# A graph network on one core: the gated layer's tables made in the attention layer's last stretches

## The chip, the cores and the metric

The kernel runs on one core of a Trainium2 chip. The metric is the device time of the whole program in microseconds (us). Five engines work side by side, each with a queue of its own: PE (matmuls; PEld are its weight loads), DVE (vector operations), ACT (activations and copies), POOL (here mostly indirect gathers) and SP (issues transfers). ACT issues transfers too. All of them synchronise by semaphores.

## The reference

Four graph layers on N = 3125 nodes with 128 features and E = 50000 edges, sorted by destination; after each, the input is added and the rows are normalised.

```python
# 0: three graph convolutions; norm = dinv[src] * edge_weight * dinv[dst]
for W, b in ((W1, b1), (W2, b2), (W3, b3)):
    x = relu(segment_sum((x @ W)[src] * norm, dst) + b)     # with a loop on each node
# 1: attention, 4 heads of 32
e = sum(leaky_relu((x @ W_l)[dst] + (x @ W_r)[src], 0.2) * att)
alpha = softmax of e over the edges of one dst
x = segment_sum((x @ W_r)[src] * alpha, dst) + bias
# 2: gated
z = concatenate([x[dst], x[src], edge_attr])
x = x + segment_sum(sigmoid(z @ W_f + b_f) * softplus(z @ W_s + b_s), dst)
# 3: ten graph convolutions, each with a layer norm and gelu, then a residual branch
```

## The kernel before

**Tiles and stretches.** The nodes are 25 tiles of 128 rows, kept in SBUF as `x`. The edges are 392 chunks of 128, cut into 28 stretches (`NS`) of 14 chunks (`SC`); a stretch has four blocks of 4, 4, 3 and 3 chunks (`BLOCKS`). Since the edges are sorted by destination, a stretch touches few rows, and after the stretches 6, 12, 18 and 24 (`WHOLE`) five more tiles (`CK`) are complete each time, 20 in all.

**Layer 0** (`l0_sorted`) is done with a dense adjacency matrix of seven banks of columns. It is built in SBUF strips out of one-hot matrices (pool `l0_hot`, tiles `of_pair`, `heavy`), used at once for the first convolution and written to memory (`bank<-strip`). The second and third convolutions stream it back in pieces of five tiles (`adj_k<-bank`, pool `l0_adj`, four buffers), which lies in SBUF where pools opened earlier have been closed. Between the two, `load_nodes` fetches `x` again and `attention.prepare` fetches and writes small things for the next layer (`s_left`, `s_dst_pad`, `wide`, `order`), all on SP.

**Layer 1**, attention (`l1_sorted`), runs as a pipeline over slots `(s, b)`, a stretch and a block of it. Its order is written out by hand: the recorders `pe_`, `ve`, `ac` and `sp` (class `InOrder`, line 189 in the profile) chain the instructions of an engine in the order in which the code issues them. POOL gathers the rows of sources (`xj`), PE brings `zT` together, ACT and DVE make `leaky`, PE the logits `e`, which go through memory (`s_logits`) to `near`; `weights` makes a maximum by scans and `w` by an exponential on ACT; `messages` (DVE, `msg`), `add_up` (PE, `sums`), `rows` and `finish` (write to `s_after`) follow three stretches later. The slots with `s >= 28` do only these last steps of the last stretches: a round is `weights(s-2)` at `b = 3`, then `messages(s-3)` at `b = 0`, `add_up` at `b = 1`, `rows` at `b = 2`, `finish` at `b = 3`. After the loop `x` is fetched again in one transfer of 25 tiles.

**Layer 2**, gated (`l2_sorted`), first prepares two tables in memory for all 25 tiles: `s2_to_src` (`row`, the product with the source's weights) and `s2_to_dst` (`parts`, the product with the destination's weights and the bias, split into three bfloat16 parts). Then it loops over the blocks of the stretches. POOL gathers `zj` from `s2_to_src` (three buffers of a stretch each; 42 gathers can run before the first buffer has to come free), PE makes `pz` out of the edges' attributes (`eaT`) and the rows of `s2_to_dst` (`td`, chosen by `of_node`, made from `drow`), DVE adds them to `z`, ACT and DVE make gate and softplus (`soft`, `gate`, `pz`), DVE `msg`, PE `sums`, and rows follow. From stretch 7 on, PE also does units of the last layer's first convolution (`sums<-adj_u,xs`, five matmuls each), added up by DVE (`columns`).

**Layer 3** (`l3`) is ten convolutions with streamed pieces of the adjacency, and isn't touched.

Of the kernel before, what the change touches and what calls it, by code (L numbers as in the profile page):

```python
# [9 lines left out]
F32 = mybir.dt.float32  # L10
# [8 lines left out]
P = 128  # L19
# [6 lines left out]
CK = 5  # L26
# [9 lines left out]
WHOLE = (6, 12, 18, 24)  # L36
CH = 20
# [11 lines left out]
def tile_gnn_stack(ctx: ExitStack, tc: tile.TileContext, a: dict, out: bass.AP):  # L49
# [96 lines left out]
    def load_nodes():  # L146
        nc.sync.dma_start(x, a["x"].rearrange("(t p) d -> p t d", p=P))
# [635 lines left out]
    def l0_sorted(edges, adj, attention):  # L783


        with (
# [13 lines left out]
            with (  # L800
                tc.tile_pool(name="l0_strips", bufs=2) as strips,
                tc.tile_pool(name="l0_hot", bufs=2) as hot,
            ):
                lanes.pin()
                edges.build(strips, hot, ps, adj, lambda b, strip: conv.sums(x, b, *layers[0], strip), ready)
                lanes.free()
            with (
# [3 lines left out]
                load_nodes()  # L811
# [249 lines left out]
    class Attention:  # L1061
# [15 lines left out]
        def prepare(self, scratch, ps, ve):  # L1077
# [11 lines left out]
            nc.sync.dma_start(self.left[NP:].rearrange("p a b -> p (a b)"), zero)  # L1089
            zero_f = scratch.tile([P, D], F32, name="zero_f")  # L1090
            nc.vector.memset(zero_f, 0.0)
            nc.sync.dma_start(self.before[NP:], zero_f)
            nc.sync.dma_start(self.after[NP - P:NP], zero_f)
            nc.sync.dma_start(self.logits[:, :NEAR], zero_f[:HEADS, :NEAR])
            nc.sync.dma_start(self.logits[:, NEAR + NCH * P:], zero_f[:HEADS, :NEAR])
            edge = scratch.tile([1, NEAR + 1], I32, name="edge")
            nc.vector.memset(edge, NP)
            nc.sync.dma_start(dst_pad[:, :NEAR + 1], edge)
            nc.sync.dma_start(dst_pad[:, NEAR + 1 + NCH * P:], edge)
            v = a["dst_r"]  # L1100
            nc.sync.dma_start(dst_pad[:, NEAR + 1:NEAR + 1 + NCH * P],
# [4 lines left out]
            nc.sync.dma_start(wide, bass.AP(tensor=dst_pad.tensor, offset=dst_pad.offset,  # L1106
# [6 lines left out]
            nc.sync.dma_start(order, bass.AP(tensor=v.tensor, offset=v.offset,  # L1113
                                             ap=[[SC, P], [SE, NS], [1, SC]]))
            v = a["src_r"]
            nc.sync.dma_start(self.src_o.rearrange("p (s c) -> p s c", c=SC), bass.AP(
# [52 lines left out]
    def l1_sorted(at):  # L1169
        right, left, before, after, local, logits = at.right, at.left, at.before, at.after, at.local, at.logits  # L1170
        fresh, src_o, dl, att, bias, apart, step = (at.fresh, at.src_o, at.dl, at.att, at.bias, at.apart, at.step)
        with (
# [5 lines left out]
            nc.vector.memset(eps, EPS)  # L1178
            with (
# [140 lines left out]

                NK = len(BLOCKS)
                load(0)
                select(0)
                for s in range(NS + 4):
                    for b in range(NK):
                        if b == 0 and s + 1 < NS:
                            load(s + 1)
# [24 lines left out]
                        if b == 3:  # L1352
                            if 0 <= s - 2 < NS:
                                weights(s - 2)
                            if 0 <= s - 3 < NS:
                                finish(s - 3)
                        if s < NS:
                            positive(s, b)
            nc.sync.dma_start(x, after[:NP].rearrange("(t p) d -> p t d", p=P))


    def l2_sorted(conv):
# [10 lines left out]
        with (  # L1373
# [7 lines left out]
            to_dst = dram.tile([NP + P, 3, 2 * D], BF16, name="s2_to_dst")  # L1381
            to_src = dram.tile([NP, 2 * D], F32, name="s2_to_src")
            before = dram.tile([NP + P, D], F32, name="s2_before")
            after = dram.tile([NP + P, D], F32, name="s2_after")
            local = dram.tile([NCH * P], BF16, name="s2_local")

# [10 lines left out]
            by_stretch = prep.tile([NS, SE], I32, name="by_stretch")  # L1397
            nc.sync.dma_start(by_stretch, a["dst_r"].rearrange("(s e) -> s e", e=SE))
            origin = one.tile([NS, len(BLOCKS)], F32, name="origin")
            lrow = prep.tile([NS, SE], BF16, name="lrow")  # L1400
            origin_i = one.tile([1, NCH], I32, name="origin_i")
            nc.sync.dma_start(origin_i, a["dst_c"][0:1, :])
            for b, (c0, n) in enumerate(BLOCKS):
                nc.vector.tensor_scalar_min(origin[:, b:b + 1], by_stretch[:, c0 * P:c0 * P + 1], float(N - 1))
                nc.vector.tensor_scalar(lrow[:, c0 * P:(c0 + n) * P], by_stretch[:, c0 * P:(c0 + n) * P],
                                        origin[:, b:b + 1], None, op0=OP.subtract)
            nc.vector.tensor_scalar(origin_i, origin_i, float(N - 1), 3.0, op0=OP.min, op1=OP.mult)
            nc.sync.dma_start(local.rearrange("(s e) -> s e", e=SE), lrow)
# [17 lines left out]
            w2 = one.tile([D, 3, 2, D], F32, name="w2")  # L1426
            for s, name in enumerate(("L2_gnn_W_f", "L2_gnn_W_s")):
                nc.scalar.dma_start(w2[:, :, s, :], a[name].rearrange("(r k) d -> k r d", k=D))
            b2 = one.tile([P, 2, D], F32, name="b2")
            for s, name in enumerate(("L2_gnn_b_f", "L2_gnn_b_s")):  # L1430
                v = a[name]
                nc.scalar.dma_start(b2[:, s, :], bass.AP(tensor=v.tensor, offset=v.offset, ap=[[0, P], [1, D]]))
# [6 lines left out]
            with tc.tile_pool(name="s2_ps0", bufs=4, space=PSUM) as ps:  # L1439
                xT = transposed_x(one, ps, conv.xs[0].rearrange("p t d -> p (t d)"))  # L1440
                def product(u, m, side):
                    pp = ps.tile([P, 2, 2 * D], F32, name="pp")[:, :m]
                    for q in range(m):
                        nc.tensor.matmul(pp[:, q, :], xT[:, (u + q) * P:(u + q + 1) * P],
                                         w2[:, side].rearrange("k s d -> k (s d)"), start=True, stop=True)
                    return pp


                for u in range(0, NT, 2):
                    m = min(2, NT - u)  # L1450
# [368 lines left out]
```

## Time and profile before

| what | value |
|---|---|
| median of 6 runs | 3546.76 us (3542.76 to 3549.2) |
| the profiled execution | 3532.18 us, span 3530.1 us |
| its mean granted clock of PE | 0.891 of full speed |
| PE busy | 2785.7 us (79% of the span) |
| DVE busy | 1645.0 us (47%) |
| ACT busy | 986.8 us (28%) |
| POOL busy | 821.1 us (23%) |
| layer 0: build and first convolution | to 364 us |
| layer 0: two streamed convolutions | to about 690 us |
| attention layer | to 1414.7 us |
| gated layer, preparation and first gathers | to 1512 us |
| gated layer, loop | to 2203 us |
| last layer | 2241 us to the end |

The profile is of one execution; it is 14.6 us shorter than the median of the runs. Times in it run from the start of the span. A line of the timeline has start, duration, engine, source line, operation, output and inputs, and in brackets how long the engine had been idle and what ended that. "issue" is idle time in which nothing that the profile shows was waited for; "remote" was ended by something that the trace doesn't hold. Source line 189 is the helper that records the hand-written order, so groups of that line are told apart by their tiles.

### The profile page before, as it was taken

Reading aid. Unit: us, or ns where it says so; the run is one execution under the profiler, and the core shown is the slowest. Engines: PE = TensorE matmul, PEld = TensorE weight load, DVE = VectorE, ACT = ScalarE, POOL = GpSimd, SP = SyncE. Lnnn points to the kernel's source line nnn. Section 1 sums busy time; section 2 is a strip of 40 time slices with the busy share of each in tenths; the row PEclk is TensorE's granted clock in tenths of the full one; section 3 lists DMA queues with packets and bytes.
Section 4 is the critical chain, followed back from the end, with each engine's and each line's share of the span. In section 5 each row is a group of like instructions: output and inputs, shape, how many; then the busy total and the mean of one; then the engine's idle time right before and its main releaser. Section 6 shows DMA issues by size and latency. Waiting matters only on the chain.

```text
span 3530.1 us, 33089 instructions
## 1 busy us (share of the span) xinstructions
PE 2785.7 (79%) x11223; PEld 1616.9 (46%) x11223; DVE 1645.0 (47%) x4368; ACT 986.8 (28%) x1491; POOL 821.1 (23%) x864
## 2 busy tenths in 40 slices
PE   2899899716656647356676677899999999999998
PEld 1666455403323324244454455455555555555554
DVE  6897112205545547466666667454232323232334
ACT  0333001202222222355555555232212122121212
POOL 3211000174555551445545452000000000000000
PEclk7899999857778778688888889999999999999999
DMA  2344987422222222655656565866766766666665
GB/s 56 113 160 163 306 278 247 152 57 78 72 68 82 80 69 60 200 157 153 204 172 200 173 193 166 265 203 200 237 208 213 227 219 221 217 215 217 223 211 176
DMA packets 413151, 609.90 MB, mean 173 GB/s; under 512 B 55434, under 2 KB 380312, under 8 KB 412956
## 3 DMA queue, kind: packets, MB, share of 16 engines
q1 hardware_dynamic: 366094, 520.33, 46.1%
q0 software_dynamic: 32320, 79.09, 8.2%
q10 hardware_dynamic: 14558, 8.27, 0.8%
q8 instruction: 91, 1.49, 0.2%
q14 instruction: 88, 0.72, 0.1%
HBM read 545.16 MB, written 62.61 MB: 172 GB/s over the span
## 4 chain that ended last, share of the span: by engine, by line
PE 44%; DVE 10%; issue 8%; another core or an unknown queue 4%; DMA 3%; ACT 1%; POOL 1%; SPq 1%; DVEq 0%; ACTq 0%
PE acc L691 34%; PE sums L189 3%; PE pz L189 3%; DVE z L189 2%; PE po L708 2%; DVE msg L189 1%; DVE pz L189 1%; DVE gate L189 1%; DVE of_edge L189 1%; PE zT L189 1%; PE e L189 1%; DMA drow<-s_local 1%; POOL xj L217 1%; SPq L189 0%
## 5 line engine op out<-in xcount | busy, mean ns | idle before, releaser
L691 PE MATMUL acc<-adj_k,xs 128*128 128x460 f32 (+1 forms) x2920 | 1120.9, 537 | 3.4 <-DMA adj_k<-bank 3.4
L691 PEld LDWEIGHTS acc<-adj_k,xs 128*128 128x128 f32 x2920 | 548.0, 190 | 503.0 <-issue 450.3
L217 POOL DMA_INDIRECT xj<-s_right,src_o x392 | 373.0, 951 | 624.5 <-ACT parts L1162 338.7
L217 POOL DMA_INDIRECT zj<-s_to_src,src_i x392 | 373.4, 953 | 364.6 <-DVE z L189 216.6
L691 PE MATMUL acc<-adj,xs 128*128 128x460 f32 (+1 forms) x1000 | 393.0, 543 | 15.2 <-DMA adj<-bank 15.2
L189 PE MATMUL pz<-w,eaT 128*128 128x256 f32 x784 | 276.2, 451 | 127.6 <-issue 97.1
L189 PE MATMUL sums<-msg,of_edge 128*128 128x132 f32 (+1 forms) x1568 | 236.0, 302 | 166.2 <-issue 138.6
L189 PEld LDWEIGHTS sums<-msg,of_edge 128*128 128x128 f32 x1568 | 214.4, 212 | 192.3 <-issue 147.5
L724 DVE SCALAR_TENSOR_TENSOR v<-po,dinv,three 128x128 f32<-128x128 f32 x250 | 72.3, 344 | 476.5 <-PE po L708 476.2
L691 PEld LDWEIGHTS acc<-adj,xs 128*128 128x128 f32 x1000 | 190.2, 191 | 202.3 <-issue 190.5
L189 PE MATMUL e<-leaky,att 128*4 128x512 f32 (+1 forms) x224 | 123.8, 638 | 148.8 <-issue 84.5
L189 PEld LDWEIGHTS pz<-w,eaT 128*128 128x128 f32 x784 | 145.8, 228 | 207.9 <-issue 135.9
L736 ACT ACTIVATE rs<-rs 128x4 f32<-128x4 f32 (+2 forms) x91 | 18.6, 205 | 681.7 <-DVE rs L735 681.6
L189 DVE TENSOR_TENSOR z<-pz,zj 128x1024 f32<-128x1024 f32 (+1 forms) x112 | 121.9, 1088 | 167.4 <-remote 139.7
L189 ACT ACTIVATE soft<-z 128x1024 f32<-128x1024 f32 (+1 forms) x112 | 106.2, 948 | 258.7 <-DVE z L189 196.6
L189 ACT ACTIVATE leaky<-zT 128x512 f32<-128x512 f32 (+1 forms) x112 | 60.5, 540 | 388.6 <-remote 184.8
L189 PEld LDWEIGHTS <-heavy 128*128 128x128 bf16 x1875 | 122.1, 101 | 83.8 <-issue 58.8
L189 PE MATMUL acc<-strip,x 128*128 128x460 f32 (+1 forms) x350 | 158.8, 562 | 0.0
L189 DVE TENSOR_TENSOR leaky<-zT,leaky 128x512 f32<-128x512 f32 (+1 forms) x112 | 69.0, 617 | 190.8 <-issue 143.0
L189 PE MATMUL side<-of_pair,heavy 128*128 128x125 bf16 x1875 | 134.6, 225 | 25.1 <-DVE heavy L189 19.7
L1710 ACT ACT_TABLE_LOAD x77 | 98.8, 1283 | 192.8 <-DVE v L1709 192.7
L189 DVE TENSOR_TENSOR heavy<-of_low,columns 128x2560 bf16<-128x2560 bf16 (+1 forms) x96 | 138.8, 1500 | 1.0
(220 smaller groups left out, 3244.5 us busy)
## 6 DMA issues: line engine op xcount, KB each, us to landing
adj_k<-bank SPq DMA_DIRECT2D x246, 1150.0 KB
adj_k<-bank SPq DMA_DIRECT2D x46, 912.5 KB
bank<-strip SPq DMA_DIRECT2D x6, 5750.0 KB
adj_u<-bank SPq DMA_DIRECT2D x24, 1150.0 KB
adj<-bank SPq DMA_DIRECT2D x14, 1150.0 KB
eaT<-in_ea_t SPq DMA_DIRECT2D x56, 256.0 KB
drow<-s_local SPq DMA_DIRECT2D x28, 448.0 KB
eaT<-in_ea_t SPq DMA_DIRECT2D x56, 192.0 KB
```

The lines of the kernel that those rows point to most:

```text
L189: ins = getattr(self.engine, name)(*args, **kwargs)
L217: after_writers(nc.gpsimd.indirect_dma_start(out=to, out_offset=None, in_=table[:NP, :], in_offset=bass.IndirectOffsetOnAxis(ap=index[:, c ...
L691: lanes.tensor.matmul(acc[:, :c1 - c0], xs[:, t, :], k[:, q, :c1 - c0], start=(t == begin), stop=(t == NT - 1))
L708: lanes.tensor.matmul(po[:, t - t0, :], self.aggT[:, t * P:(t + 1) * P], w, start=True, stop=True)
L724: lanes.vector.scalar_tensor_tensor(to[:, t - t0, :], sums[:, t - t0, :], dinv[:, t:t + 1], bias, op0=OP.mult, op1=OP.add)
L736: nc.scalar.activation(rs[:, :n], rs[:, :n], AF.Sqrt)
L1710: nc.scalar.activation(v, v, AF.Gelu)
```

## The change

There are four parts.

1. **Layer 0.** `l0_hot` is opened before `l0_strips`, so that the stream's four buffers lie in the memory of the one-hots, not of the strips. `load_nodes` and the transfers of `attention.prepare` go out on ACT's queue, not SP's.
2. **Attention layer.** A new class `Gated` holds the tables. Its weights (those of the gate negated) are fetched at the layer's start. SP fetches five finished tiles of `x` after the stretches in `WHOLE`, behind `finish`. In each slot with `s >= 28` a further pair of tiles begins its `steps`, five of them, one in each slot: transposes; the row; the bias and the product for the destination with its first part; second part; third part. They are put ahead of the attention's own work of the slot, in the same recorders, with `zT`'s buffers in PSUM and their transfers on ACT's queue. After the loop only five tiles of `x` are fetched.
3. **Gated layer, preparation.** It makes the tables of the last five tiles alone. `local`, the table behind `drow`, was written in the layer before.
4. **Gated layer, loop.** As the gate is negated, one operation over 256 columns a chunk serves gate and softplus, and ACT's exponential takes a scale of -1. `drow` comes as one transfer a stretch and `of_node` is made by one operation a stretch, at block 2. `load(s + 1)` moves from block 1 to block 0. `agg` is copied by ACT, and `u` reads PSUM. The unit is split, three matmuls at block 3 and two at the next block 0, and its addition moves from block 0 to block 1.

```diff
             with (
+                tc.tile_pool(name="l0_hot", bufs=2) as hot,
                 tc.tile_pool(name="l0_strips", bufs=2) as strips,
-                tc.tile_pool(name="l0_hot", bufs=2) as hot,
             ):
...
-                load_nodes()
+                load_nodes(nc.scalar)
...
-            nc.sync.dma_start(self.left[NP:].rearrange("p a b -> p (a b)"), zero)
+            nc.scalar.dma_start(self.left[NP:].rearrange("p a b -> p (a b)"), zero)
...
+    class Gated:
...
+        def steps(self, u, room, pe, ve, ac, queue):
+
+            m = min(2, NT - u)
+            w, pool = m * 2 * D, self.pool
+            ps = room()
+            for q in range(m):
+                pe.transpose(ps[:, q * P:(q + 1) * P], x[:, u + q, :], ident)
+            xT = pool.tile([D, 2 * P], F32, name="xT", bufs=3)
+            ac.activation(xT[:, :m * P], ps[:, :m * P], AF.Copy)
+            yield
+            ps = room()
+            for q in range(m):
+                pe.matmul(ps[:, q * 2 * D:(q + 1) * 2 * D], xT[:, q * P:(q + 1) * P],
+                          self.w[:, 1].rearrange("k s d -> k (s d)"), start=True, stop=True)
+            row = pool.tile([P, 2 * 2 * D], F32, name="row", bufs=2)
+            ac.activation(row[:, :w], ps[:, :w], AF.Copy)
+            queue.dma_start(self.to_src[u * P:(u + m) * P, :].rearrange("(t p) d -> p t d", p=P),
+                            row[:, :w].rearrange("p (t d) -> p t d", t=m))
+            yield
+            ps = room()
+            pe.matmul(ps[:, :w], self.ones, self.b.rearrange("p r s d -> p (r s d)")[:, :w],
+                      start=True, stop=False, skip_group_check=True)
+            for q in range(m):
+                pe.matmul(ps[:, q * 2 * D:(q + 1) * 2 * D], xT[:, q * P:(q + 1) * P],
+                          self.w[:, 0].rearrange("k s d -> k (s d)"), start=False, stop=(q == m - 1),
+                          skip_group_check=True)
+            parts = pool.tile([P, 2, 3, 2 * D], BF16, name="parts", bufs=3)[:, :m]
+            rest = pool.tile([P, 2, 2 * D], F32, name="rest", bufs=2)[:, :m]
+            of = ps[:, :w].rearrange("p (t d) -> p t d", t=m)
+            for i in range(3):
+                self.evict = ac.activation(parts[:, :, i], of, AF.Copy)
+                if i < 2:
+                    ve.tensor_sub(rest, of, parts[:, :, i])
+                    of = rest
+                    yield
+            queue.dma_start(self.to_dst[u * P:(u + m) * P].rearrange("(t p) i d -> p t i d", p=P), parts)
...
+                def fetch(j):
+                    sp.dma_start(x[:, j * CK:(j + 1) * CK, :],
+                                 after[j * CK * P:(j + 1) * CK * P].rearrange("(t p) d -> p t d", p=P))
...
                 for s in range(NS + 4):
                     for b in range(NK):
+                        if s >= NS:
+                            if 2 * turn < WHOLE_TILES:
+                                made.append(gated.steps(2 * turn, room, pe_, ve, ac, ac))
+                                turn += 1
+                            made = [g for g in made if next(g, made) is not made]
...
+                            if s - 2 in WHOLE:
+                                fetch(WHOLE.index(s - 2))
+                            if s == NS - 1:
+                                gated.places(ve, sp)
...
-            nc.sync.dma_start(x, after[:NP].rearrange("(t p) d -> p t d", p=P))
+            nc.sync.dma_start(x[:, WHOLE_TILES:, :], after[WHOLE_TILES * P:NP].rearrange("(t p) d -> p t d", p=P))
...
+            with tc.tile_pool(name="s2_ps0", bufs=6, space=PSUM) as ps:
+                made = [gated.steps(u, lambda: ps.tile([P, 512], F32, name="room"), nc.tensor, nc.vector,
+                                    nc.scalar, nc.sync) for u in range(WHOLE_TILES, NT, 2)]
+                while made:
+                    made = [g for g in made if next(g, made) is not made]
...
-                    ve.scalar_tensor_tensor(gate[:, :n], z[:, :n, :D], 0.0, soft[:, :n, :D],
-                                            op0=OP.min, op1=OP.subtract)
-                    ac.activation(gate[:, :n], gate[:, :n], AF.Exp)
-                    ve.scalar_tensor_tensor(soft[:, :n, D:], z[:, :n, D:], 0.0, soft[:, :n, D:],
-                                            op0=OP.max, op1=OP.add)
+                    ve.scalar_tensor_tensor(soft[:, :n], z[:, :n], 0.0, soft[:, :n], op0=OP.max, op1=OP.add)
+                    ac.activation(gate[:, :n], soft[:, :n, :D], AF.Exp, scale=-1.0)
...
-                ve.tensor_copy(agg, t["sums"])
+                ac.activation(agg, t["sums"], AF.Copy)
...
-                ve.scalar_tensor_tensor(u, t["xw"], 2.0, agg, op0=OP.mult, op1=OP.add)
+                ve.scalar_tensor_tensor(u, t["xw"], 2.0, t["sums"], op0=OP.mult, op1=OP.add)
...
-                    if b == 0 and s - 1 - FIRST in sums_of:
+                    if b == 1 and s - 1 - FIRST in sums_of:
                         add_unit(s - 1 - FIRST)
...
-                    if b == 1 and s + 1 < NS:
+                    if b == 0 and s + 1 < NS:
                         load(s + 1)
                     if k + 1 < len(steps):
                         products(*steps[k + 1])
+                    if b == 0 and s - 1 - FIRST in sums_of:
+                        unit(s - 1 - FIRST, room, range(3, CK))
...
-                    if k + 2 < len(steps):
-                        select(*steps[k + 2])
+                    if b == 2 and s + 1 < NS:
+                        select(s + 1)
...
                     if b == 3 and FIRST <= s < NS:
-                        unit(s - FIRST, ps_s.tile([P, 512], F32, name="sums"))
+                        room = ps_s.tile([P, 512], F32, name="sums")
+                        unit(s - FIRST, room, range(3))
```

## The prediction

> **What bounds the kernel now.** I read the page's slices first, then busy time by stage, then the timeline at the two seams that the change touches, then the groups and waits of the gated layer. In the slices (40 of 88 us each) PE is near full at the start and from slice 27 on; between, it is half busy and POOL, which issues the gathers, works too.
>
> ```profile
> PE   2899899716656647356676677899999999999998
> POOL 3211000174555551445545452000000000000000
> PEclk7899999857778778688888889999999999999999
> ```
>
> The last stage alone, 2400 to 3530 us, keeps PE busy for 1113.61 of 1130 us. The change leaves it as it is, so it can only win or lose before 2241 us: layer 0's turn (364 to 400), the attention layer's tail (1380 to 1415), the gated layer's preparation and first gathers (1415 to 1524) and its loop (to 2203).
>
> Stages (length; then busy time of PE, PEld, DVE, ACT, POOL with counts; granted clock, DMA share, GB/s):
>
> ```profile
> 360.00:380.00 20.00, 6.15 (x25) 3.59 (x23) 3.29 (x11) 0.48 (x1) 0.00 (x0) 0.67 0.70 175
> 380.00:400.00 20.00, 18.18 (x42) 8.72 (x43) 4.35 (x4) 0.00 (x0) 0.00 (x0) 0.90 1.07 379
> 1392.00:1402.00 10.00, 5.97 (x30) 5.78 (x30) 7.77 (x28) 0.50 (x2) 0.00 (x0) 0.67 0.13 32
> 1450.00:1500.00 50.00, 10.20 (x26) 6.71 (x25) 20.28 (x32) 20.73 (x34) 38.42 (x39) 0.59 0.63 197
> ```
>
> The turn loses PE for 14 us. The tail is nearly empty on ACT and DMA, and half empty on PE. While POOL gathers for the gated layer, the others do little. The timeline of these seams (start, duration, engine, instruction, idle time before and what ended it):
>
> ```profile
> 345.15 0.36 SPq L562 DMA_DIRECT2D bank<-strip  x1
> 363.88 0.77 SPq L147 DMA_DIRECT2D x<-in_x  x1
> 372.67 2.00 SPq L189 DMA_DIRECT2D adj_k<-bank  x1
> 380.23 6.00 PE L691 MATMUL acc<-adj_k,xs 128*128 128x460 f32 x10 [1.85 <-DMA adj_k<-bank]
> ...
> 1417.75 0.79 SPq L1359 DMA_DIRECT2D x<-s_after  x1
> 1426.41 3.84 PE L618 MATMUL xT_ps<-ident,x 128*128 128x128 f32 x16 [16.37 <-DMA x<-s_after]
> 1449.31 0.96 POOL L217 DMA_INDIRECT zj<-s_to_src,src_i  x1 [36.54 <-DVE rest L1466]
> 1511.66 1.22 DVE L189 TENSOR_TENSOR z<-pz,zj 128x1024 f32<-128x1024 f32 x1
> 1523.68 0.94 POOL L217 DMA_INDIRECT zj<-s_to_src,src_i  x1 [19.41 <-DVE z L189]
> ```
>
> From the attention layer's last write (1414.71) it takes 3.0 us until x is fetched, 8.7 until it is there, 22.9 of transposes, products and table rows until the first gather; 42 gathers then run 55 us, and 19.4 us pass before the 43rd. From there POOL sets the pace:
>
> ```profile
> 1895.58 0.96 DVE L189 TENSOR_TENSOR z<-pz,zj 128x768 f32<-128x768 f32 x1 [6.63 <-remote]
> 1900.46 0.96 DVE L189 TENSOR_TENSOR z<-pz,zj 128x768 f32<-128x768 f32 x1
> 1901.69 0.95 POOL L217 DMA_INDIRECT zj<-s_to_src,src_i  x1 [8.76 <-DVE z L189]
> ```
>
> A stretch is 14 gathers (17.2 us) and a gap: the next run waits for z of block 3, which frees the buffer, and z of block 2, 6.63 us idle before it, starts only 2.65 us after the run's end (1892.93). So a gap is 2.65 + 5.85 (z to z and its length) + 0.27 = 8.77 us.
>
> **The change part by part.** Sums are against the profiled execution, 3532.18 us; the median is 14.6 higher.
>
> *Layer 0's turn.* The stream's buffers move into the one-hots' memory, whose last reader ends at 344.42, so the first adj_k piece can be issued ahead of the bank write of 345.15, and the next three right behind it rather than after nodes and nine small transfers at 372.67. The bank write's packets end at 359.2; a piece lands every 3.15 us (1.15 MB at some 370 GB/s) and PE uses one in 3.93 (ten of 0.39). PE lost 13.85 us in the first window, 1.82 in the second and 2.1 to a cold clock (0.60 for 0.39, ten times): 17.8. I leave 5 of these, since x (1.6 MB, about 5 us), order (about 3) and wide (about 5) still share the DMA engines with the pieces, whose share was 1.07 right after: **-13** (-9 to -16). The Trainium skill's "Trainium Kernel Development and Optimization", Key Constraints, says that DMAs from the SP, ACT and POOL queues run on the same 16 engines, and that issuing from several saves only issue time; by it the move to ACT's queue is worth SP's 8.8 us from 363.88 to 372.67 at most, and the sum would be some 4 us higher. The trace's share of 1.07 agrees with it, while the memory move, which it does not touch, is the rest.
>
> *Attention layer, fetches.* Behind four of the 28 writes of finish, SP now waits for the write to land before it fetches five tiles of x. The nearest row is the 3.0 us from 1414.71 to 1417.75. Queued behind on SP are the next loads of hl and drow, and of_node waited up to 2.32 us for drow already. The stretch is 24.5 us and loads go two ahead, so I take 1 us each: **+4** (0 to +10). Its weights and indices (some 460 KB) are fetched at the layer's start, beside the first 84 gathers (704 to 802), where PE is busy for 7.92 of 50 us: nothing; without that cover, five issues of 0.5 us.
>
> *Attention layer, tail.* Ten pairs of tiles go through five steps in 14 slots from s=28 on, ahead of the attention's own work in the queues of PE, DVE and ACT. A full slot costs ACT three parts of 0.63, a row of 0.60, a copy of xT of 0.36 and two DMA issues of some 0.5 to 0.7: about 4.2 us; DVE two subtractions of 0.69; PE two transposes (0.2 each), four products and the bias product: 3.1 at full clock (0.22 a record), 6 at the cold one (0.53). A round of the old tail takes 11.9, 11.8 and 10.7 us and is a chain: msg on DVE 3.0, sums on PE 5.0 to 5.75, rows 2.2, scans 1.5, w on ACT 0.22. Half of its slots hide behind other engines: the slot before sums lies beside msg. The subtractions in the slots of rows, of weights and of msg stand in front on DVE and wait for PE and ACT: 2 to 4 us each. That makes 7 to 9 a round, less in the last, where no new pairs start: **+20**. The lower bound is ACT's own time, 10 x 4.2 = 42 for the 34 us that the tail had, less what starts in the idle time before 1380: +8. The upper is PE at its cold clock, 60 us of tables beside three times 5.4 of sums: 76 - 34 = +42.
>
> *Gated layer, preparation.* Twenty tiles' tables are already there. x's reload is 320 KB; the same size took 6 us from issue to use at 2215.84, where 1600 KB took 8.7: -2.5. Twenty-five transposes with their copies and 13 row products become five tiles in a chain of some 8 us: of 22.9 us some 10 stay, as the 1.6 MB write of s_before still shares the engines with the last rows. So the first gather comes about 15 us sooner (12 to 20). Parts now end far ahead of the gathers (1490.98 before), and drow of a stretch comes in one transfer: of_node waited 6.40 us for it until 1511.39. The gap behind the 42 gathers falls from 19.4 toward 8.77, for which I take 9 us (3 to 12): **-24** (-15 to -32).
>
> *Gated layer, loop.* Gate and softplus become one operation of 128x1024 (as z's 1.22) for 0.68 + 0.70; agg's copy of 0.28 leaves DVE for ACT; of_node's four operations of 0.35 become one of 0.69 in block 2. On the chain z to z in the gap that is -0.16, -0.28 and +0.34: -0.1. The unit's columns addition moves from block 0 to block 1, so that z of block 0 need not wait for five unit products (z at 1906.29 could come some 1.5 us sooner), and SP has three issues fewer a stretch. Much of this stands in waits. Over 25 stretches I take 0.3 each: **-8**, with -33 and +14 as ends (below).
>
> *Turn to the last layer.* The loads for it keep their order but for seven small ones that go ahead of the last writes; PE's idle time at 2241 ended on adj<-bank as before: 0 (-2 to +3).
>
> Sum: -13 + 4 + 20 - 24 - 8 = -21, so 3511 profiled and **3526** as a median.
>
> **The rivals.**
> *The tail costs more than the preparation gives (slower).* PE's clock was 0.67 at 60% busy; if it stays there, the tail is bound by PE at 6 us a slot: +42, and the last tables in the ACT ring delay the first gather, leaving -15. -13 + 4 + 42 - 15 - 8 = +10: 3557. With the preparation at -15 it decides from a tail of +32. For it: the in-order queues; against it: more work should lift the clock (1.00 at 400 to 450 us), and POOL is silent after 1342.6.
> *The loop goes into its shorter rhythm.* Some gaps are 5.4 to 7.3 us, where z of block 2 ran before the run's end (1687.62 us). With z of block 0 earlier, the 17 long gaps could lose 2 each: -33 for -8, 3501. Against it: z of block 2 waited even at 10 us after a run's start (1564.00 after 7.12).
> *The loop loses its short gaps.* The seven gaps under 8.1 sum to 13.6 us below 8.77; a chain longer by of_node's 0.69 could end them all: +14 for -8, 3548.
> *Earlier gathers serve nothing.* If PE and SP stay starved until the 42 gathers have landed and the gap behind them stays 19.4, and s_before's write holds the rows, the preparation gives 5: 3545, no change.
>
> **How the numbers follow.** Main case 0.45, with its terms' bounds 3505 to 3545: 0.40 faster, 0.05 same. Tail 0.20, slower. Short rhythm 0.15, faster. Lost gaps 0.08: 0.05 slower, 0.03 same. No use 0.12: 0.08 same, 0.03 slower, 0.01 faster. So faster 0.56, same 0.16, slower 0.28, where 0.2% (7 us) is about what a measurement of this kernel can tell from no change. The range, 3490 to 3560, holds all but the worse half of the tail's case and a short rhythm joined to a cheap tail.
>
> **What would show it.** PE's first layer-1 product soon after 366 us; rounds of msg in the tail 18 to 20 us apart, with DVE or ACT waiting for gated products; 15 us from the last write of the attention layer to the first zj gather for 34.6, and some 10 us before the 43rd gather for 19.4; gaps of about 8.5 us after. Wrong it would be if the rounds stay near 12 (gain larger) or exceed 25 (slower), or if periods in the loop move from 26 by over 1 us.

## The result and the profile after

On the chip of the profile the changed kernel takes 3515.99 us (median of 20 runs) against 3541.99 (46 runs): the ratio is 0.9929, 95% interval 0.9918 to 0.9939, which is 25 us less. Forecast were 20.8 us less. The profiled execution takes 3512.66 us (span 3510.9) for 3532.18. On a second kind of chip, told of below, the same change gains nothing: 1.0019 (1.0004 to 1.0033).

The slices of the page after (PE, POOL, granted clock):

```profile
PE   2899999726656558456777778899999999999998
POOL 3211000265556551355454541000000000000000
PEclk9999999857777779677888888999999999999999
```

PE is a tenth fuller in eight of the slices from 9 to 25, and a tenth emptier in one (the 14th); the last layer is as it was. The helper of the hand-written order is line 190 in the changed kernel, for 189 before. The stretches of before again (length; busy time of PE, PEld, DVE, ACT, POOL; clock, DMA share, GB/s):

```profile
360.00:380.00 20.00, 14.19 (x38) 6.45 (x36) 2.79 (x9) 0.00 (x0) 0.00 (x0) 0.91 1.04 298
380.00:400.00 20.00, 18.01 (x49) 9.41 (x50) 0.49 (x2) 0.55 (x1) 0.00 (x0) 0.91 1.08 377
1392.00:1402.00 10.00, 10.00 (x50) 8.00 (x51) 6.96 (x17) 4.44 (x9) 0.00 (x0) 0.83 0.50 164
1450.00:1500.00 50.00, 11.46 (x42) 7.46 (x42) 7.08 (x9) 9.35 (x12) 36.22 (x39) 0.57 0.58 174
```

In layer 0's turn PE is busy for 14.19 of 20 us, where it was 6.15. In the stretch of the attention layer's tail, where PE was busy for 5.97 of 10 us, it is now busy for all 10 (in the rest of the tail, 1334 to 1430, for 64 to 89% of the time), and ACT works there for 4.44 us and not 0.50. During the gated layer's first gathers DVE and ACT have lost most of the tables' work. The timeline at the seams:

```profile
340.14 0.36 SPq L190 DMA_DIRECT2D adj_k<-bank  x1
359.32 4.02 PE L692 MATMUL acc<-adj_k,xs 128*128 128x460 f32 x10
371.73 5.82 PE L692 MATMUL acc<-adj_k,xs 128*128 128x460 f32 x10 [2.39 <-DMA adj_k<-bank]
...
1431.25 0.40 SPq L1458 DMA_DIRECT2D x<-s_after  x1
1452.19 0.98 POOL L218 DMA_INDIRECT zj<-s_to_src,src_i  x1 [14.68 <-DMA s_to_dst<-parts]
1514.48 0.95 POOL L218 DMA_INDIRECT zj<-s_to_src,src_i  x1 [9.91 <-DVE z L190]
```

Milestones read off both timelines, in us:

| from, to | before | after | change |
|---|---|---|---|
| start to the last group of one-hot products | 344.1 | 339.8 | -4.3 |
| to the last group of products for attention's tables | 332.4 | 325.5 | -6.9 |
| to the first xj gather | 7.3 | 10.1 | +2.8 |
| to the end of the last xj gather | 658.8 | 659.3 | +0.5 |
| to the last y of the attention layer (tail) | 71.8 | 94.3 | +22.6 |
| to the first zj gather | 35.0 | 23.1 | -11.8 |
| to the 43rd zj gather | 74.4 | 62.3 | -12.1 |
| to the last run of gathers (24 periods) | 609.9 | 594.0 | -16.0 |
| to the last layer's first streamed product | 107.8 | 112.0 | +4.2 |
| to the end | 1288.7 | 1290.5 | +1.8 |

These sum to -19.2, the difference of the spans. Each column is read off one execution.

### The profile page after: what moved, and what is told of

It reads as the page before. It is cut to its first block, busy times and chain, and to the rows that moved or that the text cites. A ratio compares the mean times of both kernels' runs of the same rounds, so it can differ in the third digit from the quotient of the medians.

```text
span 3510.9 us, 32732 instructions
## 1 busy us (share of the span) xinstructions
PE 2808.8 (80%) x11249; PEld 1615.4 (46%) x11249; DVE 1597.8 (46%) x4127; ACT 1004.9 (29%) x1539; POOL 823.9 (23%) x864
## 4 chain that ended last, share of the span: by engine, by line
PE 52%; issue 9%; DVE 5%; DMA 3%; another core or an unknown queue 2%; ACT 1%; POOL 1%; SPq 0%; ACTq 0%; DVEq 0%; POOLq 0%
PE acc L692 34%; PE pz L190 7%; PE sums L190 5%; PE zT L190 2%; PE po L709 2%; DMA drow<-s_local 1%; PE e L190 1%; POOL xj L218 1%; DVE of_edge L190 1%; DMA eaT<-in_ea_t 1%; DVE msg L190 0%; ACT soft L190 0%; DVE leaky L190 0%; DVE pz L190 0%
## 5 line engine op out<-in xcount | busy, mean ns | idle before, releaser
L190 PE MATMUL pz<-w_edge,eaT 128*128 128x256 f32 x784 | 286.8, 461 | 136.8 <-issue 107.4
L725 DVE SCALAR_TENSOR_TENSOR v<-po,dinv,three 128x128 f32<-128x128 f32 x250 | 72.4, 344 | 476.5 <-PE po L709 476.2
L190 PE MATMUL sums<-msg,of_edge 128*128 128x132 f32 (+1 forms) x1568 | 216.9, 291 | 89.0 <-issue 77.3
L190 PEld LDWEIGHTS pz<-w_edge,eaT 128*128 128x128 f32 x784 | 150.5, 233 | 231.8 <-issue 183.2
L190 PEld LDWEIGHTS sums<-msg,of_edge 128*128 128x128 f32 x1568 | 198.3, 202 | 113.6 <-issue 86.3
L190 PE MATMUL zT<-ident,xj 128*128 128x128 f32 x392 | 84.1, 323 | 80.5 <-issue 57.9
```

The costliest lines, as they stand in the source:

```text
L190: ins = getattr(self.engine, name)(*args, **kwargs)
L725: lanes.vector.scalar_tensor_tensor(to[:, t - t0, :], sums[:, t - t0, :], dinv[:, t:t + 1], bias, op0=OP.mult, op1=OP.add)
```

## The experiments

Ratios are to the kernel before, run on the same chip. There were two kinds of chips, as far as the times tell. On the first, that of the profile, the kernel before takes 3543 us (l0_only, no_tables, early_pairs, block_drow; later early_load1_b and no_tables_b); on the second 3162 us (late_xw, block_load1, whole_unit, two_gates; after_again, early_load1). Each kernel is compared only within its kind.

**Layer 0's part alone (l0_only).**

```diff
+                tc.tile_pool(name="l0_hot", bufs=2) as hot,
                 tc.tile_pool(name="l0_strips", bufs=2) as strips,
-                tc.tile_pool(name="l0_hot", bufs=2) as hot,
...
-                load_nodes()
+                load_nodes(nc.scalar)
...
-            nc.sync.dma_start(self.left[NP:].rearrange("p a b -> p (a b)"), zero)
+            nc.scalar.dma_start(self.left[NP:].rearrange("p a b -> p (a b)"), zero)
...
```

> The kernel before with the first part of the change alone (the stream's buffers in the one-hots' memory, nodes and small transfers on ACT's queue). My theory: the turn from layer 0's first convolution to its second is some 7 us shorter, as in the changed kernel, of which 2 to 3 us are lost again ahead of the attention layer's first gather; with the 4 us by which the changed kernel's building of the adjacency was shorter if that comes from the pools' order, -8 in all, without it -4. Rival: all of it is lost again behind the gathers, which set the attention layer's pace: 0 to -2.

Measured: 0.9971 (0.9951 to 0.9990), -10 us. The first xj gather comes at 671.08 us for 683.81. Nothing is lost ahead of it; that loss, of 2.8 us, comes with the tables: from the end of the last product for attention's tables to the first gather it is 3.5 us in the four profiles of this kind of chip without them and 6.4 in the four with them. First l0_only, then the changed kernel:

```profile
670.45 0.38 ACTq L1167 DMA_DIRECT2D s_left<-parts  x1
671.08 0.98 POOL L217 DMA_INDIRECT xj<-s_right,src_o  x1 [330.27 <-ACT parts L1162]
```

```profile
671.99 0.38 ACTq L1168 DMA_DIRECT2D s_left<-parts  x1
674.63 0.39 ACTq L1187 DMA_DIRECT2D w<-in_L_gnn_W_f  x1
675.44 0.98 POOL L218 DMA_INDIRECT xj<-s_right,src_o  x1 [334.61 <-DMA s_left<-parts]
```

The gathers start 0.6 us after the last issue in the one, and wait for its landing, 3.45 us, in the other. The rival (0 to -2) is out. The building is shorter in every kernel with the new order of pools: 339.7 to 341.4 us to the last group of one-hot products in the seven profiles of the first kind of chip that have it, for 344.1. Two lines of the building, first before and then after, show a part of it: before, the first `of_pair` had to wait for the transfer of another tile.

```profile
75.22 1.47 DVE L189 TENSOR_TENSOR of_pair<-pairs,columns 128x2520 bf16<-128x2520 bf16 x1 [0.94 <-DMA degrees<-sums]
73.60 1.42 DVE L190 TENSOR_TENSOR of_pair<-pairs,columns 128x2520 bf16<-128x2520 bf16 x1
```

That wait of 0.94 us is gone in all seven. The eighth `of_pair` waits 3.23 us for PE before and 0.47 after, which makes 2.8 of the 4.3 us; as this wait is 2.12 us in early_load1_b, it isn't shown to hang on the order of pools.

**All but the tables' move (no_tables).** The changed kernel with the preparation of before, for 25 tiles, and nothing in the tail.

```diff
-                        if s >= NS:
-                            if 2 * turn < WHOLE_TILES:
-                                made.append(gated.steps(2 * turn, room, pe_, ve, ac, ac))
...
+            nc.sync.dma_start(x, after[:NP].rearrange("(t p) d -> p t d", p=P))
```

> The changed kernel without its second and third part: all 25 tiles' tables are made in the gated layer's preparation, as before; the stream's memory and the gated layer's loop are as changed. My theory: the tables' move gave back in the tail (+20, and +3 ahead of it) what the preparation and the first gathers gained (-24), so this kernel is as fast as the changed one, some 24 us under the kernel before, and its gated loop is about 16 us shorter than before. Rival: the loop's gain hangs on the tables being ready early; then the loop here is at most 8 us shorter and the kernel only 10 to 15 us under the one before.

Measured: 0.9918 (0.9890 to 0.9945), and a second time 0.9924 (0.9901 to 0.9947), beside 0.9929 for the whole change. So the part that the change is named after brings nothing that can be measured on this kind of chip: the tail takes 72.4 and 74.6 us and not 94.3, the first gather comes 34.4 and 35.2 us after it and not 23.1, the 43rd 71.8 and 73.2 later and not 62.3. The loop's 24 periods take 586.8 and 590.5 us, so its gain doesn't hang on the tables either. For the second time the text on record was:

> no_tables once more. On a chip like the second (kernel before 3162 us, changed kernel 1.002), it tells whether the loss there is the tables' move or the loop's edits: if the move gives back in the tail what it wins, as on the first chip, 1.000 to 1.005; if the move costs there, since the other engines aren't held back during the first gathers, 0.990 to 0.996. On a chip like the first: 0.992 again.

It fell on a chip of the first kind; what the move is worth alone on the second kind wasn't measured.

**Seven pairs earlier (early_pairs).**

```diff
-                        if s >= NS:
-                            if 2 * turn < WHOLE_TILES:
-                                made.append(gated.steps(2 * turn, room, pe_, ve, ac, ac))
-                                turn += 1
-                            made = [g for g in made if next(g, made) is not made]
+                        if 2 * turn < WHOLE_TILES and (s >= NS or (b == 0 and turn < 7 and s == 12 + 2 * turn)):
+                            made.append(gated.steps(2 * turn, room, pe_, ve, ac, ac))
+                            turn += 1
+                        made = [g for g in made if next(g, made) is not made]
```

> The changed kernel with seven of the ten pairs begun earlier: one pair at block 0 of the stretches 12, 14, ... 24, once its tiles have been fetched, and only three pairs in the tail. My theory: in the attention layer's loop POOL sets the pace and the other engines have idle time, so a pair costs there about 1 us or less, and the tail grows by some 6 us for 20: 7 to 14 us under the changed kernel. Rival: in the in-order queues each pair lengthens the chain between two runs of gathers by 3 us, as in the tail: 7 x 3 - 14 = +7 against the changed kernel.

Measured: 0.9910 (0.9886 to 0.9935), which can't be told from the changed kernel's 0.9929. The tail falls by 8 us, to 86.2, where 14 were expected. From the first xj gather to the last y the attention layer takes 748.4 us, for 753.6 in the changed kernel, and 736.8 to 743.3 in the kernels without tables on this kind of chip (730.5 before): it varies by as much as is at stake. Inconclusive on this kind of chip; early_load1, below, has the earlier pairs on the other.

**drow block by block (block_drow).**

```diff
-                    t["drow"] = drow = two.tile([3 * FEW, SE], BF16, name="drow", bufs=1)
+                    t["drow", b] = drow = ahead.tile([3 * FEW, 4 * P], BF16, name="drow", bufs=5)
...
-                    if b == 2 and s + 1 < NS:
-                        select(s + 1)
+                    if k + 2 < len(steps):
+                        select(*steps[k + 2])
```

> The changed kernel with drow fetched and of_node made for each block again, four times a stretch, as before; all else as changed. My theory: the loop's gain of 16 us (0.65 a stretch) is shared between this edit, with three issues of SP and some 0.7 us of DVE a stretch, and the unit's later addition; undone, it costs 5 to 10 us in the loop and about 4 us before the first z, where of_node waited for drow: +8 to +14 against the changed kernel. Rival: of_node's operations stood in waits, as the prediction has it: 0 to +3 in the loop.

Measured: 1.0059 (1.0036 to 1.0081), 46 us over the changed kernel and far over both expectations. The 24 periods take 638.7 us, 45 more than after and 29 more than before, which had drow in blocks too. So an order in the changed loop makes it dear. The waits of block_drow from 1700 to 2080 us (time, times, longest) and one stretch of it:

```profile
POOL zj L218 <- DVE z L190: 135.4, 14, 10.7
DVE of_node L190 <- DMA drow<-s_local: 40.4, 14, 3.8
```

```profile
1881.51 0.35 DVE L190 TENSOR_SCALAR of_node<-drow,third 126x512 bf16<-126x512 bf16 x1 [2.75 <-DMA drow<-s_local]
1883.86 1.22 DVE L190 TENSOR_TENSOR z<-pz,zj 128x1024 f32<-128x1024 f32 x1
1892.79 1.22 DVE L190 TENSOR_TENSOR z<-pz,zj 128x1024 f32<-128x1024 f32 x1
1897.95 0.96 DVE L190 TENSOR_TENSOR z<-pz,zj 128x768 f32<-128x768 f32 x1 [1.34 <-PE sums L190]
```

of_node waits for drow in each stretch, and all that follows moves back: z of block 1 runs near the end of the run of gathers (1878.16 to 1895.35) and z of block 2 after it. So two blocks, not one, are left for the gap. This holds in 23 of the 24 gaps, which are 9.3 us and longer; before, 17 of 24 were 8.7 to 9.1 us. drow is late because SP is: with `load(s + 1)` at block 0, xw's load waits for its buffer until rows has run at block 2, and all later loads stand behind it. SP's queue over the same stretch shows 14 us between two loads:

```profile
1888.67 0.01 SPq L190 DMA_DIRECT2D drow<-s_local  x1
1902.80 0.34 SPq L190 DMA_DIRECT2D xw<-s_before  x1
```

**The xw load moved (late_xw), and load(s + 1) back at block 1 with drow in blocks (block_load1).**

```diff
-                    t["xw"] = two.tile([P, D], F32, name="xw")
-                    sp.dma_start(t["xw"], before[bass.ds(t["first"], P)])
...
+                    if b == 3 and s + 1 < NS:
+                        load_xw(s + 1)
```

This is late_xw. block_load1 is block_drow's edit and one more:

```diff
-                    if b == 0 and s + 1 < NS:
+                    if b == 1 and s + 1 < NS:
                         load(s + 1)
```

> The changed kernel, with the load of xw for the next stretch (SP) moved from block 0 to block 3, behind finish's write; all else as changed. In the changed loop xw's load at block 0 waits for its buffer, which rows frees at block 2, and the loads of the next blocks (td, eaT) are queued behind it on SP. My theory: this wait holds the loop back; without it the 24 periods from the 43rd gather on fall from 594 us to 560 to 580, and the kernel by 15 to 30 us. Rival: td and eaT are loaded far enough ahead (four blocks), and only drow was late where it was loaded block by block: no change (-5 to +5).

> The kernel with drow block by block (block_drow), with load(s + 1) back at block 1 as well, as in the kernel before. My theory: block_drow was slow since drow is queued on SP behind xw's load, which waits from block 0 on for rows at block 2; of_node then waited 2.75 us for drow in each stretch, and z of blocks 1 and 2 fell behind the point from which PE starves. With the load at block 1 the wait is a block shorter and the loop's 24 periods return from 639 us to 590 to 612, the kernel to some 30 to 45 us under block_drow. Rival: the four operations and the three further issues themselves cost the time: within 10 us of block_drow.

Both ran on the second kind of chip, so the changed kernel was measured there too.

> The changed kernel itself, run beside the next one. The four kernels before this ran on a chip on which the kernel before takes 3161 us, not 3543, and the changed kernel was not among them. If it is such a chip again, my theory says 0.985 to 0.990 of the kernel before, since there POOL's gathers follow each other almost without a gap and the loop is shortened by the operations that leave DVE; the rival, that the gain hangs on the slow phases of PE, says 0.993 to 1.000. On a chip like the first: 0.993 again.

Measured there: the changed kernel 1.0019 (1.0004 to 1.0033), late_xw 0.9911 (0.9890 to 0.9933), block_load1 0.9872 (0.9851 to 0.9892). The first is worse than both expectations, which were 0.985 to 0.990 and 0.993 to 1.000. The kernel before has no profile on this kind, so where the change loses there can't be read stage by stage. PE isn't starved there; the stretch 700 to 760 us of the changed kernel, first on the first kind and then on the second:

```profile
700.00:760.00 60.00, 15.30 (x38) 4.56 (x38) 2.45 (x4) 3.31 (x5) 45.38 (x48) 0.59 0.20 54
```

```profile
700.00:760.00 60.00, 45.63 (x172) 18.62 (x171) 34.69 (x111) 20.71 (x34) 45.46 (x48) 0.80 0.37 101
```

POOL issues the same 48 gathers, and PE gets through 172 matmuls and not 38. What is left to win there is in the loop, and the waits of SP's queue from 1300 to 1750 us and its timeline name it. The changed kernel, then late_xw:

```profile
SPq L190 <- DVE st L190: 243.9, 22, 13.3
```

```profile
1511.72 0.47 SPq L190 DMA_DIRECT2D drow<-s_local  x1
1525.67 0.35 SPq L190 DMA_DIRECT2D xw<-s_before  x1
1526.59 0.39 SPq L190 DMA_DIRECT2D td<-s_to_dst  x1
```

```profile
1501.94 0.36 SPq L190 DMA_DIRECT2D eaT<-in_ea_t  x1
1512.77 0.37 SPq L190 DMA_DIRECT2D s_after<-y  x1
1513.83 0.34 SPq L190 DMA_DIRECT2D xw<-s_before  x1
1516.10 0.38 SPq L190 DMA_DIRECT2D td<-s_to_dst  x1
```

SP still waits once a stretch in late_xw, for y, but with all four blocks' loads ahead of the wait and not one block's. The zj gathers take 538.7 us from first to last in the changed kernel, 519.3 in late_xw, 502.4 in block_load1. So the position of that load costs the change some 34 us on this kind of chip (1.0019 less 0.9911, of 3162; 22 to 45 by the intervals, from two chips). The profiles show less of it: 20 us in the loop and 3.5 at the turn to the last layer. block_load1's SP waits for st too (186.2 us in the same window): what counts is not the length of the wait but what stands behind it. That block_load1 is faster still, with drow in blocks, fits of_node's waits for drow from 1240 to 1760 us, 44.5 us in the changed kernel, 34.8 in late_xw and 19.3 in block_load1. Little is left there: POOL's runs of 17.3 us with 0.3 between them would make 24 periods of some 420 us, and block_load1 takes 432.4, the changed kernel 468.8. late_xw and block_load1 weren't run on the first kind.

**The unit whole (whole_unit), and two operations for the softplus sum (two_gates).**

```diff
...
-                    if b == 1 and s - 1 - FIRST in sums_of:
+                    if b == 0 and s - 1 - FIRST in sums_of:
                         add_unit(s - 1 - FIRST)
...
-                    if b == 0 and s - 1 - FIRST in sums_of:
-                        unit(s - 1 - FIRST, room, range(3, CK))
...
-                        room = ps_s.tile([P, 512], F32, name="sums")
-                        unit(s - FIRST, room, range(3))
+                        unit(s - FIRST, ps_s.tile([P, 512], F32, name="sums"))
```

> The changed kernel with the unit of the last layer's first convolution in one piece at block 3 and its addition at block 0 again, as before. My theory: z of block 0 then waits for five unit products and for the addition (1.5 to 2 us), z of block 2 more often falls behind the point from which PE starves, and the loop's 24 periods rise from 594 to 600 to 612 us: +6 to +18. Rival: the gain of the loop is that of of_node and drow alone: 0 to +4.

Measured on the second kind: 1.0039 (1.0025 to 1.0053), the zj gathers 549.8 us. That is +6 us against the changed kernel (on another chip of the kind) with overlapping intervals, and +11 in the gathers: the direction of the theory, not proved.

```diff
-                    ve.scalar_tensor_tensor(soft[:, :n], z[:, :n], 0.0, soft[:, :n], op0=OP.max, op1=OP.add)
+                    ve.scalar_tensor_tensor(soft[:, :n, :D], z[:, :n, :D], 0.0, soft[:, :n, :D], op0=OP.max, op1=OP.add)
                     ac.activation(gate[:, :n], soft[:, :n, :D], AF.Exp, scale=-1.0)
+                    ve.scalar_tensor_tensor(soft[:, :n, D:], z[:, :n, D:], 0.0, soft[:, :n, D:], op0=OP.max, op1=OP.add)
```

> The changed kernel with the softplus sum as two operations of half the width on DVE (gate half first) instead of one. The prediction's term: two of 0.68 and 0.70 for one of 1.22, on the chain of a gap 0.16 us: +4 over the loop, at most +10 with the other blocks. Rival: the gate's exponential on ACT can start after the first half, 0.5 us sooner, which shortens the way to msg: -5 to 0.

Measured on the second kind: 1.0099 (1.0078 to 1.0120), 25 us over the changed kernel; the zj gathers take 563.6 us. Neither expected it. The trace shows a wait that came with it, here from 1240 to 1760 us:

```profile
DVE pz L190 <- ACT gate L190: 107.6, 93, 8.6
```

The second of the two operations (it writes `soft`, which lies in pz's tile) now stands behind ACT's exponential for the gate, which reads the other half of that tile, 1.2 us each time; the changed kernel has no such wait. In the kernel before the first half went into a tile of its own, `gate`, so this edit doesn't bring the old order back. That this wait makes the 25 us is likely and not tested; the prediction's 0.16 us for one operation in place of two stays untested.

**Both together (early_load1).**

> The version that the runs point to: seven of ten pairs begun in the attention layer's loop (early_pairs), drow and of_node block by block, and load(s + 1) at block 1 (block_load1). My theory: both gains add, since they lie in different stages: about 0.6% less in the attention layer's tail than the changed kernel, and in the loop as good as the changed kernel or better (on the second chip the loop's gathers from first to last took 502 us with this order against 519 with the changed kernel's and xw moved): 0.975 to 0.985 of the kernel before. Rival: on a chip where POOL's gathers starve PE, drow block by block costs what it cost in block_drow: 0.995 to 1.005.

Measured on the second kind: 0.9839 (0.9824 to 0.9854), the best there, 57 us under the changed kernel by the ratios. Most of it is the loop's order. Beside block_load1's 0.9872, on another chip of the kind, the earlier pairs add some 10 us, and the profiles show them where they were meant to be: the attention layer's tail takes 46.4 us for 61.7. Then on the first kind:

> early_load1 once more, on whatever chip this is. On one like the first (kernel before 3543 us), my theory says that drow block by block was slow in block_drow only because of the wait of xw's load ahead of it: with the load at block 1 the loop's 24 periods take 590 to 612 us for block_drow's 639, and the kernel is at 0.985 to 0.993 of the one before. Rival: the operations themselves cost it, 630 us and more, 0.998 to 1.005. On a chip like the second: 0.984 again.

Measured: 0.9958 (0.9942 to 0.9975), over the changed kernel's 0.9929. The 24 periods take 615.3 us: 23 under block_drow, so the place of `load(s + 1)` was about half of that kernel's loss; and 21 over the changed kernel (25 over no_tables the second time, on the same chip), from which it differs in the loop by both edits, drow in blocks and the load at block 1. drow once with the load at block 1 wasn't run, so the rest can't be put on drow alone. What came lies between the two expectations. Of the new versions only the changed kernel and early_load1 ran on both kinds, and each is the better one on one of them.

## Why the prediction was right, point by point

- *Layer 0's turn, -13.* Measured -11.2, but in part by luck. 4.3 of the 11.2 us lie in the building, which I had at nothing; the turn itself gained 6.9, less than the least I gave it (-9), and 7.2 to 9.3 in the six other profiles of this kind of chip that have the edit. The mechanism shows: the first piece is issued at 340.14 us, ahead of the bank write, and PE goes on with it at 359.32. The pieces behind it still come late (a wait of 2.39 us at 371.73), at a DMA share of 1.04 and 1.08. The Trainium skill's "Trainium Kernel Development and Optimization", Key Constraints, says that transfers from ACT's queue run on the same DMA engines as SP's, and that a second issuing engine saves issue time alone; the full share after the move agrees with it. No run moved the buffers without the queue, so what each of the two gave is not shown.
- *Weights at the attention layer's start, 0.* Wrong by 2.8 us: the first gather now waits for the landing of the writes before it.
- *Fetches, +4.* The layer's loop took 0.5 us more. On the first kind of chip the kernels with the fetches take 654.9 to 662.2 us there and those without 658.8 to 670.9, so no cost shows.
- *Tail, +20.* Measured +22.6, and it comes with the tables (72.4 and 74.6 us without them). The rounds of msg grow to 14.0, 17.2 and 21.5 us from 11.7 to 11.9, unevenly and not to 18 to 20 each. That the subtractions stand in front of the attention's work on DVE is the order of the code; what they wait for there shows in the waits from 1360 to 1432 us:

```profile
DVE rest L190 <- ACT parts L190: 16.8, 12, 2.3
ACT parts L190 <- PE zT L190: 9.8, 4, 4.5
```

  The clock was 0.83 with PE full (0.67 in that stretch before) and 0.86 to 0.98 beside it, so the rival of a cold, PE-bound tail (+42) did not come.
- *Preparation and first gathers, -24.* Measured -11.8 and -12.1, for -15 and -9. Where the missing 3 us can lie the timeline shows: the rows were copied from 1441.15 on, but SP issued them at 1445.44, behind three loads of indices. SP held the first of these, src_i, for 3.37 us, 2.2 of them waiting for ACT's xT (0.34 in the kernel before, where the load came earlier), and the third, origin_i, waited 2.9 us on the large write of s_before:

```profile
1437.24 3.37 SPq L1487 DMA_DIRECT2D src_i<-in_src_c  x1
1441.15 0.60 ACT L1224 ACTIVATE row<-room 128x512 f32<-128x512 f32 x1 [1.72 <-PE room L1221]
1445.09 0.25 SPq L1495 DMA_DIRECT2D origin_i<-in_dst_c  x1
1445.44 0.89 SPq L1225 DMA_DIRECT2D s_to_src<-row  x2
```

- *Loop, -8.* Measured -16: the direction was right, the sum behind it wasn't. The chain in a gap, from z of block 2 to z of block 3, was to be 0.1 us shorter; it became 0.7 longer (4.88 us before, 5.58 after, where nothing else disturbs it). Gate and softplus in one operation gave 0.18 and of_node cost 0.32, about as forecast. The step that failed is agg's copy, counted as -0.28: on ACT it stands behind the softplus, and u waits for it, so that from msg to u it takes 0.55 more. The lines are of before, before, after, and of the waits after from 1514 to 2130 us; DVE waits so in every stretch, 29.7 us in all:

```profile
1899.10 0.28 DVE L189 COPY agg<-sums 128x128 f32<-128x128 f32 x1
1899.41 0.29 DVE L189 SCALAR_TENSOR_TENSOR u<-xw,agg 128x128 f32<-128x128 f32 x1
2106.19 0.29 DVE L190 SCALAR_TENSOR_TENSOR u<-xw,sums 128x128 f32<-128x128 f32 x1 [0.79 <-ACT agg L190]
DVE u L190 <- ACT agg L190: 29.7, 24, 5.2
```

  The gain came as the second rival had it, in part: z of block 2 starts earlier. On the mean of 24 gaps it starts 0.1 us ahead of the run's end and not 1.9 after it, and in 10 of them it starts ahead, where before it did in one. (The prediction read 1687.62 as such a case; that run ends at 1686.82.) One of the ten:

```profile
2101.66 0.96 DVE L190 TENSOR_TENSOR z<-pz,zj 128x768 f32<-128x768 f32 x1 [5.66 <-remote]
2107.24 0.96 DVE L190 TENSOR_TENSOR z<-pz,zj 128x768 f32<-128x768 f32 x1
2108.47 0.95 POOL L218 DMA_INDIRECT zj<-s_to_src,src_i  x1 [6.54 <-DVE z L190]
```

  So gaps under 8 us are 13 of 24 for 6, and the mean gap is 7.45 us for 8.21, though the longest are 9.4 to 9.8 and not 8.8 to 9.1. Which edit brings z forward is known in part: with drow in blocks and load(s + 1) at block 1, but all other edits of the loop, the 24 periods take 615.3 us (early_load1_b) for 609.9 before, so the others together gain nothing that shows in one profile each. With drow once a stretch and the load at block 0 it is 594.0; with drow in blocks behind that load, 638.7. I had not asked what stands behind the load that moves to block 0. What agg's copy would give if it went back to DVE wasn't run.
- *Turn to the last layer, 0.* Measured +4.2. It comes with the load of xw at block 0. On the first kind of chip this turn takes 107.4 to 107.8 us in the three profiles with that load at block 1 (before, l0_only, early_load1_b) and 109.4 to 120.1 in the five with it at block 0; on the second, 106.4 to 107.8 where it isn't at block 0 (late_xw, block_load1, early_load1) and 109.9 to 115.0 where it is.

The forecast of the whole was near since the errors of single terms nearly cancelled: loop -8 and fetches -3.5 against some +13 in the others. That is luck. Its central step, that the tail gives back what the preparation gains, holds on this kind of chip: -24 against +22.6 and +2.8. Of its own signs, the wait ahead of the 43rd gather (9.91 us for some 10) came; the 15 us from the last write to the first gather were 22.8, and the gaps of about 8.5 us are a mean of 7.45. A period of the loop went from 25.4 us on the mean (the forecast had 26) to 24.7, less than the 1 us that it named as a sign of being wrong.

## What to carry to other kernels

Work that is moved into idle engines still stands in the queues in front of the work that sets the pace: cost it by the waits of in-order queues, not by the engines' free time, and test the move by a version with all but it. When a load is moved earlier in a queue, ask what its buffer waits for and which loads stand behind it: here one load's place was worth some 34 us on one kind of chip. When a short operation moves to another engine, ask what stands ahead of it in that engine's queue: agg's copy of 0.28 us became a wait of 0.79. A gain of less than one per cent should be measured on more than one chip.

## What the runs showed of the hardware that was not expected

The same kernel takes 3543 us on some chips and 3162 on others. Most of the difference lies in the stages with gathers: of the 347 us between the two profiles of the changed kernel, 165 lie between the first and the last xj gather (659 us against 494) and 135 between the first zj gather and the last run of them; 32 are in the attention layer's tail and 12 in layer 0's building. While POOL issues gathers back to back, PE does 38 matmuls in 60 us on the one kind and 172 on the other, with POOL as busy on both (45.4 and 45.5 us). A change of 0.7% on the one is none on the other. What makes the difference wasn't tried, and each chip of these experiments was used at one time alone, so it isn't shown that the chip makes it and not the time.
